# Issuing the exponential of a key tile's scores in slot 5 of the next unit, ahead of the turn's results, instead of in slot 6

## The chip, the cores and the metric

The kernel runs on one core of one Trainium2 chip. A core has a matrix engine (TensorE, PE in the profile), an engine for elementwise work and reductions (VectorE, DVE), one for functions such as exponential and logarithm (ScalarE, ACT), one more for elementwise work (GpSimd, POOL), and an engine that issues DMAs (SyncE, SP). Each works through its own instructions in order, and they wait for one another by semaphores. The metric is the device time of one launch in microseconds (us); lower is better.

## The reference

Eight images of 128 channels and 36 x 36 points pass through two layers, all in float32.

```python
# layer 0: convolutional attention
x = x + _L0_conv_ref(_gn(x), ...)
# layer 1: additive attention over the 1296 tokens of an image, then experts
t = _to_tokens(x)
t = t + _L1_attn_ref(_ln_t(t), ...)
t = t + _L1_ffn_ref(_ln_t(t), ...)

def _L1_attn_ref(x, mask, Wq, bq, Wk, bk, w, bw):
    q = jnp.einsum('bld,ed->ble', x, Wq) + bq
    k = jnp.einsum('bld,ed->ble', x, Wk) + bk
    t = jnp.tanh(q[:, :, None, :] + k[:, None, :, :])
    scores = jnp.einsum('bijd,d->bij', t, w) + bw[0]
    attn = jax.nn.softmax(scores, axis=-1)
    return jnp.einsum('bij,bjd->bid', attn, x)
```

Almost all the time goes into the scores of layer 1: for each pair of tokens a sum over 128 channels of w times the tanh of a sum. The kernel makes it of products: with exponentials of the queries (qf) and of the keys (kf), one matmul gives a denominator d and another a numerator n, and the score is a sum of n / d over groups of channels.

## The kernel before

**Units and slots.** The scores of an image are computed by blocks of 432 queries (three to an image, `c`) and by tiles of 128 keys (ten to an image; the eleventh has only 16 keys and stands between the fifth and the sixth). One block with one key tile is a unit; there are 264. A unit has 12 slots (the short tile 2), so 2928 slots in all, and the loop at line 1344 goes through them one by one. In slot `p` the loop issues, in this order:

1. `take_turns` (1280): results, on VectorE, ScalarE or GpSimd, of side work whose matmuls were issued earlier;
2. `denominators(p + LAG)` (1162): the matmuls of d for the slot three further on, ScalarE's logarithm of d (1177) and, for a slot alone (0, 3, 6, 9) or at the end of a pair (1 and 2, 4 and 5, 7 and 8, 10 and 11), ScalarE's exponential of minus the logarithm (1180), which is 1/d;
3. `numerators(p)` (1182): the matmuls of n;
4. `terms(p)` (1190): VectorE multiplies n by 1/d; in slots 1, 4, 7 and 10 it also adds the products up itself (`accd`), in the others GpSimd adds them (`accp`, 1218 and 1220);
5. `exps` (1234), if one is pending and its slot has come;
6. `matmul_turn` (1285), in slots 2, 5, 8 and 11 (`TURNS`): matmuls of side work, as many as a balance allows, together with those of their results that are due at once.

**The exponential of a tile's scores.** After a unit's last slot, `sums` (1224) has GpSimd add the three partial sums up (1227, 1229). The score is then complete, and `exps` takes its exponential on ScalarE (1240) into a tile `e`, which the softmax weighs. `pending` holds it until its slot has come: `p + 7`, counted from the last slot of its unit, is slot 6 of the next unit (slot 4 of the one after, where the short tile stands between).

**Side work.** Four lanes hold generators that are taken in this order: `first_of_all` (the query blocks that are needed next, 799: a matmul `pq`, ScalarE's exponential 806, GpSimd's scaling 807; and the short tile's scores), `urgent` (the weighing of a finished block, `attend`, 843), `gates` (889 to 1049) and `background` (the next image's layer 0, tokens and keys, 335 to 797). When `exps` has taken the last tile of a block, it appends `attend` to `urgent` (1244). `attend` loads four token tiles by DMA, and then has TensorE weigh the values: for each of four groups of 108 queries two products of six and of five key tiles (`pa<-xh,e`, and `pa<-xr,e` for the short tile), each followed by VectorE's additions (866 to 876). The products of a turn read the tiles `e` in the order of the keys, the last tile tenth.

Layer 0 (427) is in `background`. For one block of queries it makes ten tiles of scores (`s`, 483), takes their exponential on ScalarE (486), adds them up on GpSimd (`total`, 477), weighs the values with them by pairs of tiles (`pa<-e,vw`, 507), and at the end multiplies the sum `tot` by ones (`pt`, 498), whose reciprocal scales the result. Convolutions (`pc`, 297), value products (`pvw`, 448) and key features (`pk`, 776) are also there.

**Buffers.** d has two buffers of two banks in PSUM, so the matmuls of a slot's d wait for the logarithm two slots earlier. n and all side work share four banks, in the order of issue, so a matmul of n or of side work waits until the engine that reads the bank four further back is done. The products that GpSimd reads (`rp`) have three buffers.

The few lines that set the order:

```python
NP = len(SLOTS)                 # 12
LAG = 3
DVE_PAIRS = (1, 4, 7, 10)
TURNS = (2, 5, 8, 11)
PACE = 400
```

Of the kernel before, what the change touches and what calls it, by code (L numbers as in the profile page):

```python
# [58 lines left out]
TURNS = (2, 5, 8, 11)  # L59
# [12 lines left out]
def kernel(  # L72
# [57 lines left out]
    with ExitStack() as loop, ExitStack() as score:  # L130
# [273 lines left out]
        def conv_keys(b):  # L404
            k = convolved["k"] = big_tile("k0")
            if b == 0:
                taps["k"] = load_taps("wk_t")
            for r0, nr in KROWS:
                yield from conv_turns(
                    taps["k"], (r0, nr), 1, grid(k[:, r0 * WV : (r0 + nr) * WV], WV), True  # L410
                )
# [351 lines left out]
        def keys(b, tiles):  # L763

            xT = prepared[b][1]
            yield matmuls(1)
            for t in tiles:
                o, n = KT[t]
                first = (b, t) == (0, order[0])
                if first:  # L770
                    kf_of[0] = kfp.tile([128, NF, 128], F32, tag="kf", name="kf")
                for q0 in (0, NF // 2):
                    some = slice(q0, q0 + NF // 2)
                    pk = aux("pk1").rearrange("p (q t) -> p q t", t=128)
                    for q in range(NF // 2):
                        bmm(pk[:, q, :n], feat["a_k"][:, (q0 + q) * 128 : (q0 + q + 1) * 128],
                           xT[:, o : o + n], start=True, stop=True)
                    yield TAKE
                    if first:
                        ks = kf_of[0][:, some, :]  # L780
                    else:
                        ks = kstp.tile([128, NF // 2, 128], F32, tag="ks", name="ks")
                    nc.scalar.activation(ks[:, :, :n], pk[:, :, :n], AF.Exp)
                    kd3 = kd[b][t].rearrange("p (q t) -> p q t", t=128)[:, some, :]
                    if n == REM:

                        for x in range(2):
                            nc.gpsimd.tensor_scalar(
                                ks[:, :, (x + 1) * n : (x + 2) * n], ks[:, :, :n],
                                pairs[:, min(q0, 1), x : x + 1], None, ALU.mult,  # L790
                            )
                        nc.sync.dma_start(kd3[:, :, : 2 * n], ks[:, :, n : 3 * n])
                    else:
                        nc.sync.dma_start(kd3, ks)
                    if q0 > 0:
                        made.add((b, t))
                    yield matmuls()
# [85 lines left out]
        def gating(b):  # L883
            yield from gate_logits(b, range(NCH))
            yield from gate_tokens(b)
# [184 lines left out]
        def early_shares():  # L1070

            t = one.tile(list(xpad.shape), F32, tag="xpad", name="shares0").rearrange(
                "p a b -> p (a b)"
            )[:, :N]
            nc.sync.dma_start(t, gpair[0])
            shares_of[0] = [t[:, c * CH : (c + 1) * CH] for c in range(NCH)]
            shares_of[1] = load_pieces(
                gpair[1],
                lambda: kstp.tile([128, NF // 2, 128], F32, tag="ks", name="shares1").rearrange(
                    "p q t -> p (q t)"  # L1080
                )[:, :CH],
            )

        def first_weights():

            t = one.tile(list(xwin.shape), F32, tag="xwin", name="w0").rearrange(
                "p j n -> p (j n)"
            )
            w1s[0] = t[:, : EG * HID].rearrange("p (e h) -> p e h", e=EG)
            nc.sync.dma_start(w1s[0], weight1[:EG, :128, :].rearrange("e d h -> d e h"))  # L1090
            b1_s = t[:E, EG * HID : (EG + 1) * HID]
            nc.sync.dma_start(b1_s, weight1[:, 128, :])
            b2_s = t[:, (EG + 1) * HID : (EG + 1) * HID + O]
            for h in range(2):
                nc.sync.dma_start(b2_s[E * h : E * (h + 1)], weight2[:, HID, :])
            ffn_bias.extend((b1_s, b2_s))

        def residuals(n):

            for b in range(n):  # L1100
                load_residual(b)
                yield step()
# [28 lines left out]
        def prefetch(u):  # L1131
            if u < len(units) and u not in kf_of:
                b, c, j = units[u]
                assert (b, j) in made
                n = 128 if j < NKT - 1 else 32
                kf = kfp.tile([128, NF, 128], F32, tag="kf", name="kf")
                nc.sync.dma_start(
                    kf[:, :, :n], kd[b][j].rearrange("p (q t) -> p q t", t=128)[:, :, :n]
                )
                kf_of[u] = kf  # L1140
# [21 lines left out]
        def denominators(p):  # L1162

            if p >= len(slots):
                return
            u, k = slots[p]
            d = ps_d.tile([128, 2, 512], F32, tag="d", name="d")
            n = banks(u, k)
            products(u, k, 0, [d[:, h, :] for h in range(n)])
            g, o = group_of[p]  # L1170
            if g == p:
                alone = p in ends
                lq_of[g] = lp.tile(
                    [128, 2 if alone else 4, CH], F32, tag="lq1" if alone else "lq", name="lq"
                )
            lq = lq_of[g]
            nc.scalar.activation(lq[:, o : o + n, :], d[:, :n, :CH], AF.Ln)  # L1177
            if p in ends:
                some = lq[:, : o + n, :]
                nc.scalar.activation(some, some, AF.Exp, scale=-1.0)  # L1180
# [6 lines left out]
        def ending(u):  # L1187
            return nc.vector if u == len(units) - 1 else nc.gpsimd
# [35 lines left out]
        def sums(u):  # L1224

            s = live.pop("p")
            ending(u).tensor_add(s[:, 0, :], s[:, 0, :], s[:, 1, :])  # L1227
            d = live.pop("d")
            ending(u).tensor_add(d, s[:, 0, :], d)  # L1229
            return d  # L1230
# [49 lines left out]
        def take_turns(p, k):  # L1280
            for lane in lanes:
                if lane.due(p, False) and (k not in DVE_PAIRS or lane is first_of_all):
                    lane.run(p)
# [59 lines left out]
        pending = deque()  # L1343
        for p, (u, k) in enumerate(slots):
            b, c, j = units[u]
            rem = j == NKT - 1
            if k == 0:
                prefetch(u + 2)
                if c == 0 and j == 1:
                    if b > 0:  # L1350
                        gates.append(gating(b - 1))
                    if b == NB - 1:
                        gates.append(residuals(4))
                        first_weights()
                        early_shares()
                    if b + 1 < NB:
                        background.extend(
                            (normal(b + 1), conv_keys(b + 1), layer0(b + 1), tokens(b + 1),
                             keys(b + 1, range(NKT)))
                        )  # L1360
            take_turns(p, k)
            denominators(p + LAG)
            ns = numerators(p)
            terms(p, ns)
            if pending and pending[0][0] <= p:
                exps(p, *pending.popleft()[1:])
            last = p + 1 == len(slots) or slots[p + 1][0] != u

            if j == order[-1] and u + 1 < len(units):
                for q in NEXT_AT.get(k, ()):  # L1370
                    first_of_all.append(new_block(*units[u + 1][:2], q))
            elif j == order[-2] and last and u + 2 < len(units):
                first_of_all.append(new_block(*units[u + 2][:2], IN_TURN[0]))
            behind_rem = k == 0 and u > 0 and units[u - 1][2] == NKT - 1
            matmul_turn(
                p, k == 1 if rem else k in TURNS or behind_rem,
                lanes[:1] if behind_rem else lanes,
            )
            if last and rem:
                first_of_all.append(rem_scores(p, u, live.pop("rem")))  # L1380
            elif last:
                pending.append((p + 7, u, sums(u)))
        while pending:
            exps(p, *pending.popleft()[1:])
        take_turns(len(slots), 0)
# [226 lines left out]
```

## Time and profile before

| what | value |
|---|---|
| median of 3 runs | 6008.39 us (6008.08 to 6008.49) |
| the profiled execution | 6001.25 us |
| its span, first to last instruction | 5999.3 us |
| mean granted clock of TensorE | 0.996 |
| exponentials of line 1240 on a whole tile | 240, 640 ns each |
| logarithms of a whole slot (1177) | 2904, 879 ns each |
| exponentials of line 1180: alone, of a pair | 960 of 924 ns, 960 of 1644 ns |
| matmul records of the weighing (`pa<-xh,e`) | 1920 |
| exponentials of layer 0 (486) | 240, 521 ns each |
| GpSimd's additions (1220) | 1439, 2023 ns each |

The views name an instruction by engine, line, operation and tiles, out<-in. A line of the timeline has the start, the time and the instruction, with "x4" for four in a row; in brackets stands the idle time of its engine before it and what ended it. A matmul in float32 leaves two records. In the answer by stretches each engine has its busy time and, in brackets, its instructions, and then the clock that TensorE was granted (PEclk, 1.00 is full). The matmuls of side work all have line 279 or 283, those of the two helpers that record them, and are told apart by their tiles.

### The profile page before, as it was taken

The numbers are of one execution on the slowest core, as the hardware profiler recorded it, in microseconds if no ns is written. First come the engines' busy times: TensorE is split into PE (matmuls) and PEld (weight loads), VectorE is DVE, ScalarE is ACT, GpSimd is POOL, SyncE is SP. The second block draws the span as 40 slices with busy tenths as digits, with TensorE's granted clock in tenths as the row PEclk, the third lists the DMA queues.
The fourth block names the chain that finished last, engine by engine and source line by source line (L and its number), as shares of the span: only waits on it lengthen the run. The fifth ranks groups of instructions, "written<-read, shape, count | busy, mean of one in ns | idle before, by whom it ended". The sixth has DMA issues, their size and how long they took to land.

```text
span 5999.3 us, 94469 instructions
## 1 busy us (share of the span) xinstructions
PE 5629.9 (94%) x33507; PEld 2937.7 (49%) x33507; DVE 4780.5 (80%) x9566; ACT 5359.6 (89%) x5995; POOL 4581.9 (76%) x2870
## 2 busy tenths in 40 slices
PE   8999999999999999999999999999999999998888
PEld 5554455545554454544545445454445544544334
DVE  4787878878788788877888778887878878788884
ACT  3999999999989899889998989989998999999993
POOL 5777777877778868778788777877777777778872
PEclk9999999999999999999999999999999999999999
DMA  1200021001110011100111001110011100210007
GB/s 60 70 23 23 29 73 40 21 25 41 62 39 21 27 54 48 38 24 23 64 38 40 23 23 67 38 36 23 25 66 37 36 23 25 77 57 22 30 26 284
DMA packets 151705, 270.43 MB, mean 45 GB/s; under 512 B 45568, under 2 KB 77568, under 8 KB 151232
## 3 DMA queue, kind: packets, MB, share of 16 engines
q1 hardware_dynamic: 151008, 263.84, 13.0%
q8 instruction: 264, 4.33, 0.3%
q14 instruction: 209, 1.71, 0.1%
q10 hardware_dynamic: 224, 0.55, 0.0%
HBM read 200.15 MB, written 63.93 MB: 44 GB/s over the span
## 4 chain that ended last, share of the span: by engine, by line
PE 58%; DVE 23%; ACT 9%; issue 7%; POOL 2%; DMA 1%; DVEq 0%; POOLq 0%; ACTq 0%
PE d L1154 19%; PE n L1154 12%; DVE rp L1211 9%; PE pa L279 7%; DVE n L1205 7%; ACT lq L1177 6%; PE pc L279 5%; DVE accd L1207 4%; PE s L279 3%; PE pk L279 3%; PE pq L279 2%; PE n L1159 1%; PE d L1159 1%; POOL accp L1220 1%; ACT lq L1180 1%
## 5 line engine op out<-in xcount | busy, mean ns | idle before, releaser
L1220 POOL TENSOR_TENSOR accp<-accp,rp 128x864 f32<-128x864 f32 x1439 | 2911.2, 2023 | 962.1 <-DVE rp L1211 933.8
L1154 PE MATMUL n<-qf,kf 32*128 32x432 f32 (+1 forms) x11520 | 2996.2, 552 | 12.1 <-ACT qf L806 7.4
L1154 PE MATMUL d<-qf,kf 32*128 32x432 f32 (+1 forms) x11520 | 2777.2, 558 | 206.5 <-ACT lq L1177 197.6
L1177 ACT ACTIVATE lq<-d 128x864 f32<-128x864 f32 x2928 | 2480.1, 876 | 338.7 <-PE n L1154 252.7
L1211 DVE TENSOR_TENSOR rp<-n,lq 128x432 f32<-128x432 f32 x3912 | 2180.1, 600 | 701.0 <-PE n L1154 570.4
L1180 ACT ACTIVATE lq<-lq 128x864 f32<-128x864 f32 (+1 forms) x1944 | 2495.9, 1284 | 61.6
L1154 PEld LDWEIGHTS d<-qf,kf 32*128 32x128 f32 (+1 forms) x11520 | 1029.1, 184 | 1359.6 <-ACT lq L1177 997.1
L1154 PEld LDWEIGHTS n<-qf,kf 32*128 32x128 f32 (+1 forms) x11520 | 1259.9, 185 | 667.0 <-issue 286.8
L1207 DVE TENSOR_TENSOR accd<-n,accd 128x432 f32<-128x432 f32 x1440 | 866.1, 601 | 24.6
L1205 DVE TENSOR_TENSOR n<-n,lq 128x432 f32<-128x432 f32 x1440 | 809.4, 607 | 47.2 <-PE n L1154 29.0
L1218 POOL TENSOR_TENSOR accp<-rp 128x864 f32<-128x864 f32 x240 | 485.2, 2022 | 250.8 <-DVE rp L1211 250.0
L1229 POOL TENSOR_TENSOR accd<-accp,accd 128x432 f32<-128x432 f32 x239 | 265.0, 1109 | 18.7
L279 PE MATMUL pa<-xh,e 128*108 128x129 f32 x1920 | 251.0, 280 | 30.0 <-DVE accd L1207 28.7
L279 PEld LDWEIGHTS pa<-xh,e 128*108 128x108 f32 x1920 | 220.2, 173 | 118.3 <-DVE accd L1207 97.4
L1227 POOL TENSOR_TENSOR accp<-accp 128x432 f32<-128x432 f32 x239 | 263.7, 1103 | 12.2
L807 POOL TENSOR_SCALAR qf<-qf,cs_s 128x432 f32<-128x432 f32 x192 | 260.1, 1364 | 4.1 <-ACT qf L806 4.0
L477 POOL TENSOR_TENSOR tot<-tot,e 116x432 f32<-116x432 f32 x192 | 211.7, 1103 | 16.6 <-ACT e L486 13.2
L279 PE MATMUL s<-q,k 128*116 128x432 f32 x480 | 209.6, 548 | 9.5 <-DVE accd L1207 7.5
L279 PE MATMUL pa<-e,vw 116*128 116x432 f32 x480 | 200.8, 541 | 0.0
L279 PEld LDWEIGHTS pk<-xT,a_k 128*128 128x128 f32 x1408 | 165.6, 193 | 57.9 <-DVE accd L1207 42.8
L486 ACT ACTIVATE e<-s 116x432 f32<-116x432 f32 x240 | 118.8, 521 | 83.5 <-PE s L279 80.8
L279 PE MATMUL pk<-xT,a_k 128*128 128x128 f32 (+1 forms) x1408 | 180.7, 281 | 2.4 <-DVE accd L1207 1.3
(260 smaller groups left out, 3754.6 us busy)
## 6 DMA issues: line engine op xcount, KB each, us to landing
kf<-kd SPq DMA_DIRECT2D x239, 512.0 KB
kd<-ks SPq DMA_DIRECT2D x158, 256.0 KB
w<-in_weight_dram SPq DMA_DIRECT2D x32, 1024.0 KB
wk_t<-wk_t_d SPq DMA_DIRECT2D x7, 768.0 KB
wv_t<-wv_t_d SPq DMA_DIRECT2D x7, 768.0 KB
wq_t<-wq_t_d SPq DMA_DIRECT2D x7, 768.0 KB
x<-in_x_dram SPq DMA_DIRECT2D x8, 648.0 KB
t<-tokd SPq DMA_DIRECT2D x96, 54.0 KB
```

The source lines that it names most:

```text
L279: mm(out, lhsT, rhs, **kw)
L807: nc.gpsimd.tensor_scalar(qf[:, 1, :], qf[:, 0, :], feat["cs_s"][:, q : q + 1], None, ALU.mult)
L1154: mm(outs[h][:, :CH], kf[rows[h], q, :], qf_of[b, c, q][rows[h], part, :], start=True, stop=True)
L1177: nc.scalar.activation(lq[:, o : o + n, :], d[:, :n, :CH], AF.Ln)
L1180: nc.scalar.activation(some, some, AF.Exp, scale=-1.0)
L1205: mult(ns[h], ns[h], lq[:, o + h, :])
L1207: nc.vector.tensor_add(live["d"], ns[h], live["d"])
L1211: mult(rp[:, h, :], n, lq[:, o + h, :])
L1218: nc.gpsimd.tensor_add(live["p"], live["r"], rp)
L1220: ending(u if k == NP - 1 else 0).tensor_add(live["p"], live["p"], rp)
L1227: ending(u).tensor_add(s[:, 0, :], s[:, 0, :], s[:, 1, :])
L1229: ending(u).tensor_add(d, s[:, 0, :], d)
```

## The change

The pending exponential is due at `p + 6` instead of `p + 7`, and it is issued only in a slot that has a matmul turn. From the last slot of a unit, `p + 6` is slot 5 of the next unit. Where the short tile stands between, `p + 6` is slot 3 of the unit after it, which has no turn, so it becomes slot 5 there too (it was slot 4). Within slot 5 the exponential is issued after the logarithm and the exponential of slots 7 and 8 and before the turn's matmuls and their results.

```diff
             denominators(p + LAG)
             ns = numerators(p)
             terms(p, ns)
-            if pending and pending[0][0] <= p:
+            if pending and pending[0][0] <= p and k in TURNS:
                 exps(p, *pending.popleft()[1:])
...
             elif last:
-                pending.append((p + 7, u, sums(u)))
+                pending.append((p + 6, u, sums(u)))
```

On ScalarE the instruction moves from behind the exponential of slot 9 (line 1180) to in front of the results of turn 5 and of the logarithm of slot 9. Because `exps` also appends `attend`, the weighing of a finished block begins in the turn of slot 5 of the next block's first tile, where it began in that of slot 8. The work that stood in that turn, and what follows it in the lower lanes, is moved by a turn or more: in the third image, for instance, the turns of the first unit of the second block hold

| slot | before | after |
|---|---|---|
| 2 | two convolution groups (`pc`) | the value products (`pvw`) |
| 5 | two convolution groups | weighing, 6 and 5 products |
| 8 | weighing, 6 products | weighing, 6 products |
| 11 | weighing, 5 and 6 products | weighing, 5 and 6 products |

and the product with `tot` of that image's second block in layer 0 moves from slot 2 of the third block's first unit to slot 2 of its third unit. The number of instructions of each kind is the same.

## The prediction
> **What bounds the kernel now.** I read the page's busy shares first, then the two tables of waits (TensorE's, ScalarE's), then three stretches of the timeline. The shares name no winner:
>
> ```profile
> PE 5629.9 (94%) x33507; PEld 2937.7 (49%) x33507; DVE 4780.5 (80%) x9566; ACT 5359.6 (89%) x5995; POOL 4581.9 (76%) x2870
> ```
>
> The waits show two engines taking turns: who waited, for whom, us in total, times, longest.
>
> ```profile
> PE d L1154 <- ACT lq L1177: 197.6, 395, 2.0
> PE pt L279 <- POOL tot L477: 19.9, 9, 3.1
> ...
> ACT lq L1177 <- PE n L1154: 252.7, 312, 2.9
> ...
> ACT e L1240 <- DVE accd L1229: 5.8, 1, 5.8
> ```
>
> TensorE waits 395 times for ScalarE's logarithm to free a bank for d, and ScalarE 312 times for TensorE. The timeline of ScalarE alone, where no matmul turn has work, shows why:
>
> ```profile
> 3006.01 0.92 ACT L1180 ACTIVATE lq<-lq 128x864 f32<-128x864 f32 x1
> ...
> 3010.97 0.92 ACT L1180 ACTIVATE lq<-lq 128x864 f32<-128x864 f32 x1
> 3011.80 0.64 ACT L1240 ACTIVATE e<-accd,eb_s 128x432 f32<-128x432 f32 x1
> 3012.35 1.65 ACT L1177 ACTIVATE lq<-d 128x864 f32<-128x864 f32 x2
> 3014.03 1.64 ACT L1180 ACTIVATE lq<-lq 128x1728 f32<-128x1728 f32 x1
> ...
> 3016.48 0.92 ACT L1180 ACTIVATE lq<-lq 128x864 f32<-128x864 f32 x1
> ```
>
> Three slots take 4.96 us (3006.01 to 3010.97) with ScalarE never idle; with the moved exponential among them 5.51 us. So it costs **0.55 us** where ScalarE is the bound. Where a turn's matmuls are long, the first logarithm behind them waits, and ScalarE idles there: that idle time can cover the exponential. Before the change it stands behind the exponential of slot 9, so the turn of slot 8 can cover it; after it, it stands behind that of slots 7 and 8, so the turn of slot 5 can. The cover is not new, it is another one.
>
> **Part (a): the exponential itself.** 240 of them, 0.64 us each, none added or removed. Its input is in no danger: in the trace the last sum (L1229) ends 4.0 to 8 us ahead of the new place (239 cases). For the 191 that stand at slot 6 and aren't a block's first tile I took ScalarE's idle time before the logarithm of slot 9 (cover by turn 5) and before that of the next slot 0 (cover left by turn 8): 109 have neither, no change; 26 have only the first, and gain it up to 0.55 each, 12.6 us in all; 13 have only the second: the logarithm of slot 9 comes 0.55 later, so do d of slot 11 and turn 8 behind it, which was the late one; with what is short where both are there, 13.8 us lost. Sum **+1 us**, ends -13 and +14. The results of turn 5 (key exponentials, query exponentials, s) come 0.55 later; the numerators that wait for their banks stand ahead of d of slot 11, which waits for the later logarithm anyway.
>
> **Part (b): the weighing starts one turn earlier, behind its own last exponential.** The exponential of a block's last tile appends attend() to the urgent lane. That now happens in slot 5 ahead of its turn, so this turn takes the first 11 products, of which the 10th reads that very tile. It happens at 23 block changes. Before, they stood in turn 8:
>
> ```profile
> 1601.56 0.63 PE L1154 MATMUL d<-qf,kf 32*128 32x432 f32 x2
> ...
> 1602.32 1.64 ACT L1180 ACTIVATE lq<-lq 128x1728 f32<-128x1728 f32 x1
> ...
> 1603.87 0.87 ACT L1177 ACTIVATE lq<-d 128x864 f32<-128x864 f32 x1
> ...
> 1605.60 0.64 ACT L1240 ACTIVATE e<-accd,eb_s 128x432 f32<-128x432 f32 x1
> ...
> 1606.45 2.46 PE L279 MATMUL pa<-xh,e 128*108 128x129 f32 x20
> ...
> 1610.09 0.89 ACT L1177 ACTIVATE lq<-d 128x864 f32<-128x864 f32 x1 [0.61 <-PE n L1154]
> ```
>
> Here the exponential is done (1606.24) before the products begin. After: numerators of slot 5 end at 1601.55, the products start at about 1601.6 (20 records in 2.46 us, so 0.25 a product), and nine are through at 1603.9. The exponential then starts as that of slots 7 and 8 ends (1603.96) and lands at 1604.5: TensorE waits 0.65 us, and d of slot 9 behind it. Two products (0.5) and d with its tail (0.75, as from 1609.3 to 1610.05) put the logarithm of slot 9 at 1606.0 instead of 1603.87, 2.1 us late, of which the moved exponential fills 0.55. The next turn (6 products) can't start before VectorE frees a bank: it gets the five results of the weighing (1.2 us) ahead of the terms of slot 6, so I put the next logarithm of slot 0 at 1612.1 instead of 1610.09: +2.0. The four turns behind it then hold 1.5, 0.1, 1.1 and 0 us of idle time instead of 0.8, 1.5, 0.1 and 1.1: -0.8. So **+1.2 us each, 28 us**. Lower end: if VectorE does not hold the next turn, 0.1 each, +2; upper end: the whole idle time of 1.6 us with nothing back, +37. Every DMA of attend() (four loads of 54 KB on SP's queue) goes one turn earlier too; nothing stands behind them but the next tile's keys, needed a unit later: nothing.
>
> **Part (c): a wait on GpSimd that goes away.** As the weighing takes turn 5, the work of the background lane behind it moves. One piece matters: the product with tot (line 498). In images 1 to 6 it stands in slot 2 at the start of the third block, behind the unit in which GpSimd also scales eight query blocks (1.36 us each):
>
> ```profile
> 2084.65 1.36 POOL L807 TENSOR_SCALAR qf<-qf,cs_s 128x432 f32<-128x432 f32 x1
> 2085.98 1.09 POOL L477 TENSOR_TENSOR tot<-tot,e 112x432 f32<-112x432 f32 x1
> ...
> 2087.13 0.99 PE L279 MATMUL pt<-tot,ones 116*128 116x432 f32 x2 [3.10 <-POOL tot L477]
> 2087.96 3.04 PE L279 MATMUL pa<-e,vw 116*128 116x432 f32 x4
> ```
>
> TensorE stands still for 3.1 us, six times. In the changed order slot 2 there holds two s products, and this one comes two units later, six slots behind its last addition and past the crowded unit. ScalarE's idle time behind the six was 3.14 us three times and 4.8 three times, 23.9 in all; elsewhere 0.03 to 0.19 stands behind such a turn: **-23 us**. Next late is GpSimd's own sum (done at 2089.3, wanted at about 2092.5): no wait. Ends -24 and 0 (it waits in its new place). The 4.8 are the clock: after three of the waits the products ran at a granted clock of 0.72, after the others at 1.00:
>
> ```profile
> 1362.00:1368.00 6.00, 5.86 (x28) 2.76 (x30) 3.28 (x7) 3.51 (x5) 5.10 (x5) 1.00 0.00 0
> ...
> 2087.00:2093.00 6.00, 5.87 (x22) 2.66 (x22) 1.86 (x4) 1.91 (x3) 4.19 (x4) 0.72 0.00 0
> ```
>
> [...]
>
> **Part (d): other turns regrouped.** I took the mean idle time behind each kind of turn in this trace and counted the kinds in both orders. Up: 12 more turns with two weighted products alone (0.73 each), the value products in one turn instead of three (6 times 1.1), 12 more with one query block and two products (0.56), and smaller ones, +26. Down: fewer s, weighted and query mixtures, -18. Sum **+8 us**, those two as ends.
>
> **The sum.** 1 + 28 - 23 + 8 = +14 us: 6001.25 for the profiled execution becomes 6015; the median shown, 6008.39, stands 7.1 above it, so **6022**.
>
> **Rivals.** *Faster*: (c) pays and (b) is at its lower end, because VectorE frees the bank in time and the second turn swallows the wait: 1 + 2 - 23 and (d) at nothing, 5988. It wins once (b) costs less than 0.6 us a block change. For it: the wait is only 0.65 us, and TensorE already waits 0.5 us on average at each of 395 places without the span following each. Against: the three-slot stretch has no idle time to give back. *Nothing to be seen*: the terms cancel, 6008. *Much slower*: the product with tot waits in its new place too, and (b) is at its upper end: 6008 + 1 + 37 + 0 = 6046. For it: GpSimd is busy throughout the crowded unit; against: the next two units bring it no query block. *It doesn't do what it says*: the sum isn't ready at the new place, so ScalarE stalls in each unit; a wait of 0.5 us would give 240 x 0.5, 6128. The 4.0 us to spare speak against it.
>
> **How the numbers follow.** Forecast 0.42, faster 0.23, nothing 0.13, much slower 0.18, not ready 0.04. A measurement tells 0.2%, 12 us, from no change. Of the forecast, whose own spread is +4 to +30, 0.27 lies above 12 us; with 0.18 and 0.04 slower is 0.49. Faster is 0.20 of the second case. The rest, 0.31, is the same. The range reaches from the faster case to the much slower one with the unknown ends cut at both sides: 5988 to 6048.
>
> **What would show it.** Right: the first logarithm behind turn 5 of a block's first tile about 2 us later, with TensorE waiting for the exponential of line 1240 some 23 times; the nine waits of 19.9 us for tot down to two or three; the exponential with no wait for line 1229. Wrong: waits of TensorE for line 1240 that sum to 15 us with the span unchanged (then (b) is hidden), or waits for tot in the new place.

## The result, and the profile after

| | before | after |
|---|---|---|
| median, measured side by side | 6008.18 us (6006.62 to 6008.49) | 6043.88 us (6041.82 to 6048.38, 6 runs) |
| ratio, 95% interval | | 1.006 [1.0049, 1.0071] |
| the profiled execution | 6001.25 us | 6048.38 us |
| its span | 5999.3 us | 6046.7 us |
| mean granted clock | 0.996 | 0.991 |
| stretches at a granted clock of 0.50, most of them 3.41 us long | 47.4 us in 11 places | 113.0 us in 27 places |

The change costs **35.7 us**, 0.6%. The forecast was 6022, +14: the sign and the range (5988 to 6048) held, and 22 us of the loss were not in the sum. The profiled execution of after lies 4.5 us above its median and that of before 7 below, so the two profiles differ by 47.3 us; the experiments below, not this difference, carry the sizes.

The shares of the page hide it. Every engine but TensorE is as busy as before, and TensorE's 37.5 us more are the same 33507 instructions taking longer:

```profile
PE 5667.4 (94%) x33507; PEld 2963.0 (49%) x33507; DVE 4779.5 (79%) x9566; ACT 5357.5 (89%) x5995; POOL 4583.2 (76%) x2870
```

The waits of the changed kernel (who waited, for whom, us in total, times, longest) answer to those shown of before:

```profile
ACT lq L1177 <- PE n L1154: 264.7, 297, 2.6
PE d L1154 <- ACT lq L1177: 225.7, 421, 2.4
ACT lq L1177 <- PE d L1154: 106.5, 96, 2.5
PE pa L279 <- ACT e L1240: 19.4, 25, 1.4
ACT e L1240 <- DVE accd L1229: 5.8, 1, 5.8
PE pt L279 <- POOL tot L477: 3.9, 13, 0.9
```

Three of the announced signs are there. TensorE now waits for the exponential of line 1240 in front of a weighing product (`pa`): 25 times, 0.78 us each, where 23 times 0.65 were announced. The waits of `pt` for `tot` fell from 19.9 us to 3.9, though in 13 short waits where two or three were announced. And the exponential waits for its sum (L1229) as little as before, so that the input is ready in its new place. A fourth sign was not announced: TensorE's waits for the logarithm rose from 197.6 to 225.7 us and ScalarE's for d from 65.5 to 106.5. The line of before for the latter:

```profile
ACT lq L1177 <- PE d L1154: 65.5, 56, 1.9
```

The block change that the prediction worked out is here in the changed kernel. TensorE and ScalarE in order of time (start, duration; in brackets the idle time before and what ended it):

```profile
1614.12 2.24 PE L279 MATMUL pa<-xh,e 128*108 128x129 f32 x18
1614.96 1.65 ACT L1180 ACTIVATE lq<-lq 128x1728 f32<-128x1728 f32 x1
1616.51 0.64 ACT L1240 ACTIVATE e<-accd,eb_s 128x432 f32<-128x432 f32 x1
1617.20 0.47 PE L279 MATMUL pa<-xh,e 128*108 128x129 f32 x2 [0.84 <-ACT e L1240]
1618.65 0.89 ACT L1177 ACTIVATE lq<-d 128x864 f32<-128x864 f32 x1 [1.50 <-PE n L1154]
...
1624.71 0.89 ACT L1177 ACTIVATE lq<-d 128x864 f32<-128x864 f32 x1 [0.97 <-PE n L1154]
```

Nine products (18 records), then the wait, then the tenth. This unit begins at 1588.44 in the trace of before and at 1601.08 here, so the logarithm of slot 9 is 2.14 us later within its unit (1618.65 against 1603.87) and that of the next slot 0 is 1.98 later (1624.71 against 1610.09); 2.1 and 2.0 were worked out.

### The profile page after: what moved, and what is told of

Its sections match the earlier page's. It is cut to its first block, busy times and chain, and to the rows that moved or that the text cites. A ratio compares the mean times of both kernels' runs of the same rounds, so it can differ in the third digit from the quotient of the medians.

```text
span 6046.7 us, 94467 instructions
## 1 busy us (share of the span) xinstructions
PE 5667.4 (94%) x33507; PEld 2963.0 (49%) x33507; DVE 4779.5 (79%) x9566; ACT 5357.5 (89%) x5995; POOL 4583.2 (76%) x2870
## 4 chain that ended last, share of the span: by engine, by line
PE 51%; DVE 19%; ACT 16%; issue 10%; POOL 3%; DMA 0%; DVEq 0%; SPq 0%; POOLq 0%; ACTq 0%
PE d L1154 17%; ACT lq L1177 11%; PE n L1154 11%; DVE rp L1211 8%; PE pa L279 6%; DVE n L1205 5%; PE pc L279 5%; DVE accd L1207 3%; PE s L279 3%; ACT lq L1180 2%; PE pk L279 2%; POOL accp L1220 1%; ACT e L1240 1%; PE pq L279 1%; PE d L1159 1%
## 5 line engine op out<-in xcount | busy, mean ns | idle before, releaser
L1154 PE MATMUL d<-qf,kf 32*128 32x432 f32 (+1 forms) x11520 | 2804.2, 559 | 233.2 <-ACT lq L1177 225.7
L1154 PEld LDWEIGHTS d<-qf,kf 32*128 32x128 f32 (+1 forms) x11520 | 1042.9, 184 | 1382.0 <-ACT lq L1177 997.3
L1154 PEld LDWEIGHTS n<-qf,kf 32*128 32x128 f32 (+1 forms) x11520 | 1275.5, 185 | 662.9 <-issue 286.2
L1229 POOL TENSOR_TENSOR accd<-accp,accd 128x432 f32<-128x432 f32 x239 | 265.3, 1110 | 18.8
```

What stands on the lines that cost most here:

```text
L1154: mm(outs[h][:, :CH], kf[rows[h], q, :], qf_of[b, c, q][rows[h], part, :], start=True, stop=True)
```

## The experiments

Each kernel is compared with the kernel before on the same chip. The kernel before had a median of 6007.4 beside the first four, 6008.5 beside the second four, 6008.4 beside the next three and 6009.8 beside the last. Three causes were up for the loss: the weighing's wait (W, step b), the exponential's own new place (E, step a) and the side work that was moved (S, steps c and d).

### 1. The exponential alone

In the changed kernel, a finished block's weighing is put into its lane only behind the turn of slot 5. It begins in turn 8 as before the change, and no side work of images 1 to 6 moves.

```diff
             if len(es[b, c]) == NKT:
-                urgent.append(attend(b, c, es.pop((b, c))))
+                finished.append(attend(b, c, es.pop((b, c))))
...
             matmul_turn(
...
+            urgent.extend(finished)
+            finished.clear()
```

> The exponential is issued in slot 5 ahead of the turn's results, as in the changed kernel, but a finished block's weighing is handed to the urgent lane only behind that turn, so it begins in turn 8 as before and all side work of images 1 to 6 stands where it stood before. Theory W (the weighing's wait behind its own last exponential is the loss; the exponential's own place is worth +1, between -13 and +14): 6002 to 6016, likeliest 6009; half-clock stretches about the 11 of before. Theory E (the exponential's own place costs, because with the pair's exponential it keeps the d banks closed for 3.1 us, and the matrix engine's wait of 1.53 us there halves the clock): 6020 or more, with 15 or more half-clock stretches. Theory S (the regrouped side work costs): 6009, as W.

Measured: **6044.35 us** (6035 to 6049), ratio 1.0056 [1.0043, 1.0069]. As much as the whole change, with neither the weighing's wait nor, in images 1 to 6, moved side work: E alone can cost 37 us, where step (a) had +1. Three things are in it. In the first unit of nine blocks the exponential no longer stands behind the long turn of the weighing: +0.52 to +0.55 us each. Step (a) had left the first units out, rightly for the changed kernel, where the weighing stands in turn 5 and covers it. In the first unit of the third block of images 1 to 6 the product with `tot`, which still stands there, waits 3.66 to 3.98 us where it waited 3.1, and these six units are 5.1 us longer together; the changed kernel does not have this wait:

```profile
PE pt L279 <- POOL tot L477: 22.8, 7, 4.0
```

And 34 stretches at half clock stand in the trace, where before has 11: the 23 units that have such a stretch in this trace alone (three of the six are among them) are 21.9 us longer in all.

### 2. The weighing without its wait

In the changed kernel, the second part of the first group of queries, the one that reads the fresh tile, waits for the next turn. The first six products stay in turn 5, and the side work behind is moved as in the changed kernel.

```diff
                     if some[0] == 0:
                         nc.vector.tensor_copy(sums, pa)
-                        yield matmuls()
+                        yield matmuls(3 if i == 0 else 0)
```

> The changed kernel, but the second group of products of a block's weighing, the one that reads the tile just finished, is held back three slots, into turn 8; the first group stays in turn 5. The 19 us of waits for line 1240 should be gone. Theory W: the 2.0 us that a block's first unit lost go with them, less what the next unit gave back (0.7), 23 x 1.3: 6014, between 6005 and 6022. Theories E and S: 6035 or more, since the exponential's place and the moved side work stay.

Measured: **6017.6 us** (6011 to 6028), ratio 1.0017 [1.0008, 1.0026]: 26.3 us under the changed kernel. In its trace the wait is all but gone, and the waits for `tot` are no longer than 0.9 us, as in the changed kernel:

```profile
PE pt L279 <- POOL tot L477: 7.4, 18, 0.9
...
PE pa L279 <- ACT e L1240: 2.2, 2, 1.3
```

So W is worth 26 us (28 predicted). It also leaves +10 us for all the rest, where the prediction had -14.

### 3. The product with tot later, in the kernel before

```diff
                         total(NDT - 1)
-                        yield matmuls(3)
+                        yield matmuls(12 if b > 0 and c == NCH - 1 else 3)
```

> The kernel before, but the product with tot of the third block in layer 0 is put off by nine slots, past the unit in which GpSimd scales eight query blocks, so that what follows it in the background moves too, nearly as in the changed kernel. By step (c) of the prediction the six waits of 3.1 us and the half clock behind three of them go: 6008 - 23 = 5985, between 5984 and 5990. If GpSimd's backlog only shows elsewhere (rival): 6008. If the moved side work itself costs, as theory S has it: 6000 or more though the waits are gone.

Measured: **6004.85 us** (6001.5 to 6011.4), ratio 0.9997 [0.9988, 1.0006]. No gain to be told from none, though the unit with the wait became 4.6 us shorter in the mean: two units later (`pt` now stood in the last turn of the unit between, `px` and the products `po` in this one), 3.0 us were lost in the images without a stretch at half clock there (2 of 6) and 4.4 in those with one. What (c) takes away is given back when `pt` and its followers move. Experiments 9 and 12 take this up.

### 4. The exponential behind the turn's results

The changed kernel, with `exps` called behind `matmul_turn`, so that the results of turn 5 go ahead of it on ScalarE. The weighing begins in turn 8.

```diff
-            if pending and pending[0][0] <= p and k in TURNS:
-                exps(p, *pending.popleft()[1:])
             matmul_turn(
...
+            if pending and pending[0][0] <= p and k in TURNS:
+                exps(p, *pending.popleft()[1:])
```

> As the first of these runs, but the exponential is issued in slot 5 behind the turn's results instead of ahead of them; the weighing begins in turn 8. If the place in front of the results matters (their banks come free 0.55 us later), this is faster than the first run by up to 10 us; if only the covers by turns 5 and 8 count (W): the same within 6 us. Theory E: as slow as the first run, since the logarithm of slot 9 stands behind it just the same.

Measured: **6029.32 us** (6022.6 to 6039.1), ratio 1.0035 [1.0023, 1.0048]. Behind the results it costs 15 us less than ahead of them (experiment 1), with 23 stretches at half clock against 34. The intervals overlap, so the size is rough.

### 5 to 8. The same with TensorE kept busy

E had two readings: the half clock is its cost (C), or later logarithms and closed banks cost the same at full clock (B). To part them, a matmul that nothing reads was put into each turn that has no side work, in four kernels: by the records of the traces 176 times in the kernel before, 178 with experiment 1, 183 in the changed kernel, 173 with experiment 2.

```diff
+            work = behind[0]
             matmul_turn(
...
+            if not rem and k in TURNS and behind[0] == work:
+                mm(aux("idle")[:, :256], ones, feat["a_k"][:, :256], start=True, stop=True)
```

> The kernel before with one more product, 256 columns wide, whose result nobody reads, in each matmul turn that has no side work (178 of them), so that the matrix engine stays busier where ScalarE is the bound. It is the control for the next three. Theory C (the half clock is what the exponential's new place costs): the few half-clock stretches of turn-free units go (those behind the waits for tot stay): 6000 to 6008. If the added product itself costs, up to 178 x 0.55 = 98 us more: 6106.

> The exponential alone moved (the first experiment, 6044), with the same added product in turns without side work. Theory C: within 10 us of its control, so 6000 to 6018, with under half of the 34 half-clock stretches. Theory B (the new place costs at full clock too, because the logarithm of slot 9 and the bank that it frees come 0.55 us later): 6035 or more, the stretches gone or not.

> The changed kernel with the added product. Theory C: the half-clock stretches fall from 27 to under 15; what stays is the weighing's wait (26 us by the difference between the changed kernel and the run with the second group held back) less the wait for tot: 6008 to 6024. Theory B: 6038 or more.

> The changed kernel with the second group of the weighing held back to turn 8 (6018) and the added product. Theory C: its half-clock stretches go too, so it falls below the kernel before: 5985 to 6003. Theory B: 6012 to 6020.

| | without the filler | with it | ratio with it |
|---|---|---|---|
| kernel before | 6008.18 | 6022.2 | 1.0023 [1.0014, 1.0032] |
| the exponential alone | 6044.35 | 6038.89 | 1.0052 [1.0039, 1.0066] |
| changed kernel | 6043.88 | 6048.75 | 1.007 [1.0057, 1.0083] |
| weighing without its wait | 6017.6 | 6022.55 | 1.0025 [1.0016, 1.0034] |

The filler costs 14 us in the kernel before, so only differences between kernels that have it are read. In the order of the table it leaves 14, 13, 17 and 16 places at half clock, nearly level; in time they are 57, 69, 79 and 82 us. Among kernels with it the exponential alone costs 16.7 us, not 37; the weighing's wait 26.2, as without it; and **the rest of the change 0.35**, where 10 were left without it. So about 20 of the 37 us of experiment 1, and about 10 of the 36 of the change, go with the half clock (C). Of the other 16.7, by the traces with the filler, 5.3 are ten first units at 0.52 to 0.54 and 7.9 the six first units with the longer wait for `tot`, two costs that the changed kernel does not have. The step from "goes with" to "is" rests on the filler doing nothing else, which its own 14 us forbid to take as exact.

### 9. The addition into tot on VectorE, in the kernel before

Here the wait of (c) is removed in its place, with no side work moved: the last of the additions into `tot` of a third block of layer 0 goes to VectorE (7 instructions).

```diff
-                def total(j):
+                def total(j, engine=nc.gpsimd):
...
-                    nc.gpsimd.tensor_add(tot[:n], of[:n], ex[j][:n])
+                    engine.tensor_add(tot[:n], of[:n], ex[j][:n])
...
-                        total(NDT - 1)
+                        total(NDT - 1, nc.vector if b > 0 and c == NCH - 1 else nc.gpsimd)
```

> The kernel before, with one of the additions into tot moved from GpSimd to VectorE: the last one of a third block of layer 0 in images 1 to 7 (7 instructions). No side work moves to another turn. Theory (the -23 of step (c) was there to be had, and the change gave it back by what it moved into turn-free units): the waits of pt for tot (9, 19.9 us) fall to about three of 1 us or less, the unit they stand in becomes 2.5 us shorter where the clock was kept and 4.1 where it was halved behind the wait, nothing is given back two units later, about -18 us in all: 5990 (5984 to 5996), ratio 0.997. Rival (the wait covered something that has to be paid anyway, as moving pt in the kernel before showed, -4.6 in place and +3.5 two units later): within 4 us of 6008. If VectorE's addition delays a product of terms instead, 0.6 us each, 4 us of the gain go.

Measured: **5983.01 us** (5981.36 to 5984.95), ratio 0.9959 [0.9947, 0.9972]. It beats both kernels, the one before by 25 us where 18 were expected. In the timeline and the answer by stretches the product, which had stood 3.10 us, follows at once, and the clock stays full where it was 0.72:

```profile
2084.91 0.99 PE L279 MATMUL pt<-tot,ones 116*128 116x432 f32 x2
2085.74 1.61 PE L279 MATMUL pa<-e,vw 116*128 116x432 f32 x4
```

```profile
2087.00:2093.00 6.00, 6.00 (x34) 2.53 (x35) 5.27 (x10) 5.86 (x8) 5.84 (x5) 1.00 0.00 0
```

The unit with the wait is 2.97 us shorter in the three images where the clock had been kept and 4.43 to 4.65 in the three where it had been halved, 22.5 in all, and no other unit of images 1 to 6 moves by more than 0.15 in the mean. So step (c) priced its wait rightly (-23), and it was to be had. The change did not get it.

### 10. The fresh tile first

The changed kernel, with the tile whose exponential was just issued first among the products of the first group, not tenth.

```diff
-                    parts = (range(6), range(6, NKT))
+                    parts = ((9, 0, 1, 2, 3, 4), (5, 6, 7, 8, 10)) if i == 0 else (range(6), range(6, NKT))
...
-                    if some[0] == 0:
+                    if len(parts) == 2 and some is parts[0]:
```

> The changed kernel, with the key tile whose exponential has just been issued placed first among the first group's products, not tenth; the sums are the same ones in another order. Theory W (the weighing's wait for its own last exponential is the loss of step (b)): nine products (2.25 us) no longer stand in front of the wait, so it grows from 0.78 to about 3.0 us at some 23 block changes: +2.2 each, of which 0.2 to 0.5 may be given back in the next unit, +40 to +52: 6084 to 6096, and more (0.8 to 1.5 us each) where a stretch at half clock follows. Rival (the loss comes from the weighing standing in an earlier turn, whatever it waits for): 6044, no change.

Measured: **6123.82 us** (6122.05 to 6128.02), ratio 1.0195 [1.0181, 1.0209]: 80 us over the changed kernel, where 40 to 52 were expected. The wait grew to 2.85 us each, by 2.08:

```profile
PE pa L279 <- ACT e L1240: 71.3, 25, 3.6
```

Of the 23 units of a block change, 7 kept the clock and became 2.00 us longer (1.99 to 2.01), nearly the whole of the added wait. The other 16 got a stretch at half clock and became 3.69 longer. W has its price: the longer wait in front of the weighing went nearly one for one into the span (2.00 of 2.08 us). The 1.7 us on top are the price of the half clock.

### 11. The addition into tot on VectorE, in the changed kernel

The edit of experiment 9, in the changed kernel.

> The changed kernel with the same 7 additions into tot on VectorE. Theory (in the changed kernel the waits for tot are gone by place already: 13 of 3.9 us, the longest 0.9): 6040 to 6045. Rival (the waits that are left keep the units with pt long): 6028 to 6036.

Measured: **6048.22 us** (6045.81 to 6051.55), ratio 1.0067 [1.0053, 1.0081]. The same as the changed kernel. What was worth 25 us in the kernel before is worth nothing here: no long wait is left to be removed, as step (c) said.

### 12. The products behind it held back

Experiment 9, with `px` held back until `px`, the three functions of the tanh on ScalarE and the products `po` stand in the very turns where the changed kernel has them. `pt` stays in its place, without a wait.

```diff
-                    yield matmuls()
+                    yield matmuls(27 if j0 == NDT and b > 0 and c == NCH - 1 else 0)
                 px = aux("px1")
```

> The kernel with the additions into tot on VectorE, with the product px of a third block of layer 0 (and with it the three exponentials and logarithms of the tanh and the products po) held back by 27 slots in images 1 to 7: px, po and the transpositions behind them then stand in the very turns of the third block's third to fifth unit where the changed kernel has them, while pt stays in the first unit with no wait. Theory (the gain of (c) was given back because these instructions on ScalarE left the block change, where the long turns of the weighing cover them, for units with hardly a turn, in which ScalarE is never idle): the third and fourth unit grow by 2 to 3 us each, by 1.5 more where a stretch at half clock follows, the first unit gains about 0.5 to 1: +15 to +28 for six images, 5998 to 6011 against 5983 without the hold. Rival (what was given back came from pt itself and its sums in the new place, or from the work behind): 5983, no change.

Measured: **5991.75 us** (5985.92 to 5998.09), ratio 0.9966 [0.9954, 0.9978]: 8.7 us over experiment 9, where 15 to 28 were expected, and not even these come from where the theory has them. In the third block of images 1 to 6, against experiment 9, the first unit gains 1.78 us, the next five lose 2.9 in the mean and the last five gain 0.8: +0.3 an image. Most of the rest of the 11.6 us by which the two profiles differ goes with stretches at half clock in other blocks (20 in all against 8). So `px` and its followers alone are **not** the cause. Nor were the three functions covered in the first unit: they take 1.76 us, and without them it is 1.78 shorter.

Experiment 3 against experiment 9 is the other half: neither has the wait, and in experiment 3 `pt` moves as well as what follows it. There the third unit is 2.99 us longer in the two images without a stretch at half clock in it (3 and 5) and 4.3 to 4.4 in the other four; the first unit is 1.68 shorter in three images and, where a stretch at half clock stands in it, hardly shorter. Over the whole block this makes 1.9 and 1.5 us for images 3 and 5 and 3.7 to 4.6 for the other four, 20.7 in all, about the 21.8 between the medians. About 10 of them are there at full clock (1.7 an image), and as much again comes with the half clock (2.6 more in four images).

For the change itself, experiment 2 stands against experiment 9: without the weighing's wait and without the wait for `tot`, both. In the third blocks of images 1 to 6 the first unit is 0.86 us shorter, the next five are 5.5 longer and the last five 0.8 shorter, +3.8 an image, **23 us, as much as (c) was worth**. The moved exponential is in these 23 as well: alone (experiment 1 against before) it makes units two to six of these blocks 1.6 us longer an image, and how the two add up is not shown. The third unit is 2.60 longer in each image; the fifth 0.8 in three images and 3.73 in the three that have a stretch at half clock in it.

What can stand in the new place is seen at the end of the third unit of such a block in the changed kernel, in the trace of ScalarE and TensorE, and by stretches:

```profile
2161.70 1.65 ACT L1180 ACTIVATE lq<-lq 128x1728 f32<-128x1728 f32 x1
2163.25 0.55 ACT L422 ACTIVATE hpre<-hpre 128x432 f32<-128x432 f32 x1
2163.70 0.87 ACT L1177 ACTIVATE lq<-d 128x864 f32<-128x864 f32 x1
...
2164.62 1.17 PE L1154 MATMUL d<-qf,kf 64*128 64x432 f32 x4 [1.90 <-ACT lq L1177]
```

```profile
2161.91:2165.32 3.41, 1.51 (x12) 0.61 (x11) 2.70 (x6) 3.38 (x4) 3.29 (x3) 1.00 0.00 0
2165.32:2168.73 3.41, 3.41 (x8) 1.18 (x5) 1.45 (x3) 3.38 (x4) 1.24 (x2) 0.50 0.02 5
```

The last function of the tanh (line 422) stands between two logarithms of a ScalarE that is busy 3.38 of 3.41 us. The logarithm behind it is late, TensorE waits 1.90 us for it, is busy for only 1.51 us of that stretch, and is granted 0.50 in the next. Before the change the same three functions stood in the block's first unit, among the turns of the weighing, the first of them behind 0.63 us of idle time:

```profile
2097.89 0.56 ACT L416 ACTIVATE hpre<-hpre 128x432 f32<-128x432 f32 x1 [0.63 <-DVE hpre L522]
```

The moved exponential does the same by itself, here in a unit of the changed kernel whose turns 2 and 5 have no side work:

```profile
2515.14 0.64 ACT L1240 ACTIVATE e<-accd,eb_s 128x432 f32<-128x432 f32 x1
2515.68 0.87 ACT L1177 ACTIVATE lq<-d 128x864 f32<-128x864 f32 x1
2516.60 1.57 PE L1154 MATMUL d<-qf,kf 64*128 64x432 f32 x4 [1.53 <-ACT lq L1177]
```

```profile
2516.60:2520.00 3.40, 3.40 (x9) 1.45 (x10) 1.20 (x3) 3.37 (x4) 1.70 (x1) 0.54 0.00 0
```

## Why the prediction was right in sign and short in size

| step | predicted | runs |
|---|---|---|
| (b) the weighing waits for its own last exponential | +28 | +26.3 (changed kernel against 2), +26.2 with the filler |
| (c) the waits for `tot` go | -23 | -22.5 in place (9); given back in the same blocks: 20.7 when `pt` is moved alone with what follows it (3 against 9), 23 with the exponential moved too (2 against 9) |
| (a) and (d), the exponential's place and the other turns | +9 | +10 (2 against before, with (c) taken at nothing); 0.35 with the filler |
| sum | +14 | +36 |

**(b) was right in mechanism, place and size.** Experiment 2 takes the wait away and 26 us with it (it also moves what is left of the weighing by a turn); experiment 10 moves nothing to another turn, lengthens the wait, and the span follows. The rival "faster" needed this to cost less than 0.6 us a block change, and it costs 1.1 (26.3 / 23). Against that rival stood the stretch in which ScalarE is never idle, which has nothing to give back; that argument held.

**(c) is the term that failed.** Its wait was found, priced as it then measured, and is gone from the changed kernel, as the step said. "Next late is GpSimd's own sum: no wait" looked for the next wait of the same product only. The step had to ask what moves with that product: `pt` sets off two functions on ScalarE (0.51 and 0.56 us), `px` three (1.76 together), and then come the products `po`. They leave the block change for units in which ScalarE has little idle time (1.1 of 21.5 us in the third unit of image 3's third block, before the change); the third unit then grows by 2.6 to 3.0 at full clock. That moving them gives back 20.7 of the 22.5 us is shown by experiments 3 and 9; why is not. That the 2.8 us of functions are the reason is read from the timeline above, and experiment 12 speaks against it as the whole reason: the three functions that it moved were not covered in the first unit either, and they added 0.52 to the third (whose transpositions went on to the fourth) and, in five of six images, 1.5 to the fourth, which got a stretch at half clock. Whether it is `pt` with its two functions, all five together, or the products and the banks that they close stays open.

**The half clock is in it.** Step (c) saw the clock at 0.72 behind three of the six waits of 3.1 us (a stretch at 0.50 behind each of the three), and the sum has no term for the clock behind any new wait. The weighing's waits needed none: they are 0.78 us in the mean, and none of the 23 units of a block change has such a stretch in the changed kernel. But nothing asked for the clock behind the waits of 1.5 to 1.9 us that (a), (c) and (d) bring, and 16 more stretches stand in the trace of after. With the filler the rest of the change is worth 0.35 us, without it 10: about 10 of the 36 us, and about half of what (c) gave back, go with the half clock.

**(a) and (d) came out at the size of their sum by luck.** The exponential alone costs 37 us (1) where +1 was worked out: some 20 go with the half clock, which step (a) did not ask for, and 13 are first units that in the changed kernel are covered by the weighing or have lost their wait. And the +10 are there without the filler; with it 0.35 is left. "Not ready" is excluded: the exponential's one wait for line 1229 is the same 5.8 us in both traces.

What stays open: by what part of the moved work (c) is given back, how the 10 us of (a) and (d) divide, and how exact the share of the half clock is, since the filler that takes it away has a cost of its own.

## What to carry to other kernels

Where an edit moves a lane of side work, price the new place of each piece and of what it sets off some slots later, not only the wait that it leaves: what goes away in one place (here 22.5 us) can come back almost whole in others (20.7). Here the wait was better removed where it stood, by moving one small instruction to an engine that had time (VectorE, busy for 80% of the span before; 7 additions: 6008 to 5983 us), than by reordering what is around it. And before calling a new wait harmless, ask how little TensorE then does in the 3.4 us around it, since behind the weighing's waits of experiment 10 the half clock came after the emptiest of them (16 of 16 that were 12 to 38% busy, 0 of 7 at 45% or more).

## What the runs showed of the hardware

In these traces the granted clock falls to 0.50 for stretches of 3.41 us (some last 6.83 or 10.24) that lie on a raster: the 11 stretches in the trace of before begin whole multiples of 3.4133 us apart, to within 0.01 us, and so do the 27 in that of after; all 51 of experiment 10 begin at the same phase of such a period. The 23 waits of experiment 10 in front of the weighing are of one kind (2.88 to 3.56 us), and differ in where they fall on the raster. By stretches, first one that falls into one period, then one that straddles two:

```profile
2618.96:2622.37 3.41, 0.41 (x3) 0.41 (x4) 1.77 (x4) 2.92 (x3) 2.37 (x2) 1.00 0.00 0
2622.37:2625.78 3.41, 3.41 (x18) 3.41 (x17) 0.29 (x1) 0.00 (x0) 0.55 (x1) 0.50 0.00 0
...
5564.70:5568.10 3.40, 1.72 (x8) 0.69 (x8) 2.61 (x5) 3.34 (x4) 3.32 (x3) 1.00 0.00 0
5568.10:5571.50 3.40, 2.02 (x18) 2.02 (x19) 0.29 (x1) 1.33 (x2) 2.92 (x2) 1.00 0.00 0
```

At these 23, a period in which TensorE was busy 12 to 38% was followed by the half clock in 16 of 16 cases; where the wait was cut in two by the raster, so that both periods were 45% busy or more, it was not in 7 of 7. In units with other matmuls the border is not so sharp: in the changed kernel the clock also fell behind periods most of which were 43 to 61% busy (44% in the stretch at 2161.91 shown above), and in the kernel before some of 44 to 58% passed. The share of time is therefore not the whole measure; what else counts, no run here settles. The wait of 1.90 us, in a period in which TensorE was busy for 1.51 of 3.41 us, and the one of 1.53 us, in a period 55% busy (1.89 of 3.42 us from 2513.48), each had a stretch at 0.50 behind it; the weighing's 23 waits of 0.57 to 1.38 us at the block changes of after had none.

One such stretch costs 1.7 us behind a weighing (3.69 against 2.00 in experiment 10), 1.4 in the third unit of experiment 3 (4.39 against 2.99) and 0.76 behind the moved exponential alone (the fourth unit of a third block in experiment 1 is 1.30 longer with such a stretch and 0.54 without).
